# A two-layer decoder on one core: four units' context keys and values made while the router works, and three smaller edits

## The chip, the core and the metric

The kernel runs on one NeuronCore of a Trainium2 chip, as one program in one launch. The metric is the device time of an execution in microseconds (us); lower is better. A profiled execution also gives the span, from the first to the last instruction of the program on the engines.

## What is computed

The input is x, 32 sequences of 128 tokens of width 256, in f32. Each of six blocks adds its result to x:

```python
x = x + L0_attn(layernorm(x))            # latent attention, 16 heads
x = x + L0_xattn(layernorm(x), ctx, ...) # attention over ctx, with distances and a mask
x = x + L0_ffn(layernorm(x))             # 8 experts, the top 2 for each token
x = x + L1_attn(layernorm(x))            # gated scan and an MLP
x = x + L1_xattn(layernorm(x), ctx)      # attention over ctx
x = x + L1_ffn(layernorm(x))             # quantized, ternary weights, 3-tap convolution
```

What the change moves belongs to the fifth block: `lang_key = ctx @ W_lk.T + b_lk` and `lang_value = ctx @ W_lv.T + b_lv`. They depend on the inputs alone, so they may be made at any time before layer 1 reads them.

## The kernel before

**Stages.** x stays in SBUF for the whole run. `attention` (L248) does both attentions of layer 0 and, group by group of four sequences, the routing logits (`route`, L555). `phase_c` (L696) turns these into a plan for the experts, gathers tokens and runs the experts. `layer1` (L978) runs 16 units of two sequences (256 tokens) in a hand-written software pipeline (`PLAN`, a new unit every `STEP` = 11 rounds).

**The router** (L696 to L820). Two matmuls (`counts` and `totals`, L712 and L714) add up who chose which expert (`both`, written at L591). A chain of small VectorE instructions makes from them the experts' ranges, the expert of each of 71 columns of 128 tokens (`after`, `of`, `of_i`, L766 to L777), and each token's slot (`sl`, `col`, `rowp`, L764 to L785). Then 64 matmuls on one-hot tiles `onr` (L791) and `onc` (L795, scaled by ScalarE at L799) write `tokens` (L800), from which `who` and `whither`, the indices of the gathers and scatters, are made (L805 to L820).

**Contexts** (`context`, L638). One unit's context takes three pieces: `load` brings cT, 256 columns of the transposed context; `keys` is four f32 matmuls, which TensorE executes as eight instructions (tile `ck`), and two ScalarE activations that add the bias and write one half of the tile `kvc`; `values` is again eight TensorE instructions (`cv`), one VectorE add of a bias row and the store to the scratch tensor `ckv`. Of 16 units, 6 are made between the router and the experts (L829), 5 after the experts (L930), 5 within layer 1. `kvc` has four buffers, cT five. Their weights are loaded at L704 into `wc`.

**Experts.** 40 items in a list, in the repeated order of two items of two columns (256 tokens) and one of one column, two short items in a row never. `brought` (L839) reads the item's expert from `of_i`, loads its weights in two parts on SyncE's queue (tiles `moe0`, 1024 KB, and `moe1`, 1156 KB, two buffers each) and gathers the tokens on GpSimd's queue. `tokens` transposes them (PSUM `xs`, copied to `xTs` by VectorE), `first_layer` makes `h` and `second_layer` makes `y`, which a scatter on GpSimd's queue takes to `ys`. In pass j of the loop the weights of item j + 1 are asked for. At j = 1 stand the loads of layer 1's weights, `wd` (`load_d`, L688: two transfers of 1792 KB) and `wf` (L915, 2048 KB). At j = 3 stand `ternary` (L935), which adds up |wf| on VectorE, divides and rounds, and four ScalarE scalings of `wd` (L926). `wd` lies in the buffer that layer 0's weights, `wab` (L107), hold before.

**Order.** A scheduler orders each engine's instructions by its own simulated times, so one that is ready early may move ahead of others in the program. `mm` and `turned` (L206 and L209) pin a TensorE instruction behind all that was written before it for that engine with `tc.keep_in_program_order`; so do the stores to `ckv` and the fetches of `yr` on SyncE's queue. The matmuls at L712, L714, L800 and L945, the loads of `wd` and `wf`, and almost all work of the other engines are free. An instruction on an engine or queue waits at its head for all that it needs, and what is behind it waits too.

**Rows of scales** (`on_rows`, L1084). To lay 128 per-token scales along the free axis, a matmul takes the scale column, broadcast to 128 columns, as weights and the identity as moving operand; two calls for each unit, two blocks each.

Of the kernel before, what the change touches and what calls it, by code (L numbers as in the profile page):

```python
# [10 lines left out]
F32 = mybir.dt.float32  # L11
# [6 lines left out]
P = 128  # L18
# [58 lines left out]
def decoder(ctx: ExitStack, tc: tile.TileContext, a: dict, out: bass.AP):  # L77
# [28 lines left out]
    nc.sync.dma_start(out=rv, in_=a["rv"][:RV_A].partition_broadcast(P))  # L106
    wab = wpool.tile([P, AB_W], F32, tag="w1", name="wab")  # L107
    nc.sync.dma_start(out=wab[:, :A_W], in_=a["wab"][:, :A_W])
    for g in range(1, NG):
        load_x(g)  # L110
    nc.sync.dma_start(out=wab[:, A_W:], in_=a["wab"][:, A_W:])
    qpos_i = const.tile([P, NB], I32, name="qpos_i")
# [128 lines left out]
    def conr(name):  # L241
        at, w = C_AT[name]
        return cstr[:, at - C_W : at - C_W + w]

    def attention():  # L248
        with tc.tile_pool(name="pa", bufs=2) as pool, tc.tile_pool(name="pa1", bufs=1) as keep:
# [363 lines left out]
            for _ in group_a(0):  # L613
                pass
            slots = (
                (a_scores, 0), (b_scores, 0), (ahead, 0), (a_weights, 1), (b_turned, 2),
# [20 lines left out]

    def context(u, wcs, turned_tile, kv_tile):  # L638

        wc = wcs.rearrange("p (w c m) -> p w c m", w=2, c=2)  # L640
        t = {}

        def load():
            t["cT"] = turned_tile(f"cT_k{u}")
            nc.sync.dma_start(
                out=t["cT"], in_=a["ctxT"][:, u * T : (u + 1) * T].rearrange("(c p) t -> p c t", p=P)
            )

        def keys():
            t["kv"] = kv_tile(f"kvc_{u}")  # L650
            p = bank(f"ck_{u}").rearrange("p (c t) -> p c t", c=2)
            for c in range(2):
                for k in range(2):
                    mm(p[:, c, :], wc[:, 0, k, c * P : (c + 1) * P], t["cT"][:, k, :], k == 0, k == 1)
            for c in range(2):
                A.activation(
                    t["kv"][:, 0, c * T : (c + 1) * T], p[:, c, :], AF.Identity, bias=vec("b_lk")[:, c : c + 1]
                )

        def values():  # L660
            p = bank(f"cv_{u}").rearrange("p (i d) -> p i d", i=U)
            for i in range(U):
                for c in range(2):
                    mm(p[:, i, :], t["cT"][:, c, i * S : (i + 1) * S], wc[:, 1, c, :], c == 0, c == 1)
            V.tensor_tensor(
                t["kv"][:, 1].rearrange("p (i d) -> p i d", i=U), p,
                row("b_lv")[:, None, :].to_broadcast([P, U, D]), ALU.add,
            )
            tc.keep_in_program_order(nc.sync.dma_start(out=ckv[u], in_=t["kv"]))

        return load, keys, values

    CTX_FIRST, CTX0 = 6, 11

# [13 lines left out]
    def load_d():  # L688
        w = wpool.tile([P, D_W], F32, tag="w1", name="wd")
        for k in range(2):  # L690
            h = D_W // 2
            nc.sync.dma_start(out=w[:, k * h : (k + 1) * h], in_=a["wd"][:, k * h : (k + 1) * h])
        return w


    def phase_c():  # L696


        with (
# [11 lines left out]
            bothf = both.rearrange("p t e -> p (t e)")  # L711
            PE.matmul(pc[:, : NB * NE], lhsT=upper, rhs=bothf, start=True, stop=True)  # L712
            pt = bank("totals")
            PE.matmul(pt[:, : NB * NE], lhsT=ones_b, rhs=bothf, start=True, stop=True)  # L714
            k = lambda name, sh, dt=F32: keep.tile([P, *sh], dt, name=name)
# [49 lines left out]

            after = pool.tile([P, NHC * TS], F32, tag="hTs", name="after")[:, : 2 * NE * NJ]  # L766
            after = after.rearrange("p (q e) -> p q e", e=2 * NE)
            V.tensor_tensor(
                after, conr("iota")[:, :NJ, None].to_broadcast([P, NJ, 2 * NE]),
                ends.rearrange("p k e -> p (k e)")[:, None, :].to_broadcast([P, NJ, 2 * NE]), ALU.is_ge,  # L770
            )
            of, of2 = k("of", (NJ,)), k("of2", (NJ,))
            V.tensor_reduce(of, after, AX.X, ALU.add)
            V.tensor_scalar(of2, of, float(NE), -float(NE), ALU.is_ge, ALU.mult)
            V.tensor_tensor(of, of, of2, ALU.add)
            of_i = k("of_i", (NJ,), I32)
            V.tensor_scalar(of_i, of, float(NE - 1), None, ALU.min)  # L777
# [10 lines left out]
            for t in range(0, NB, G):  # L788
                for j in range(2):
                    o = pool.tile([P, G, P], F16, tag="onr", name=f"onr_{t}_{j}", bufs=3)  # L790
                    V.tensor_tensor(  # L791
                        o, conr("iota")[:, None, :].to_broadcast([P, G, P]), bc(rowp[:, j, t : t + G], P), ALU.is_equal
                    )
                    c = pool.tile([P, G, NJ], F16, tag="onc", name=f"onc_{t}_{j}", bufs=3)
                    V.tensor_tensor(  # L795
                        c, conr("iota")[:, None, :NJ].to_broadcast([P, G, NJ]), bc(col[:, j, t : t + G], NJ), ALU.is_equal
                    )
                    for i in range(G):
                        A.activation(c[:, i, :], c[:, i, :], AF.Copy, scale=conr("tok")[:, t + i : t + i + 1])  # L799
                        PE.matmul(  # L800
                            pk[j][:, :NJ], lhsT=o[:, i, :], rhs=c[:, i, :],
                            start=t + i == 0, stop=t + i == NB - 1,
                        )

            two = k("two", (2, NJ))  # L805
            for j in range(2):
# [13 lines left out]
            V.tensor_copy(whither, tkn)  # L820

            contexts = [
                context(
                    u, wcs, lambda n: cpool.tile([P, 2, T], F32, tag="cT", name=n, bufs=5),
                    lambda n: cpool.tile([P, 2, U * D], F32, tag="kv", name=n, bufs=4),
                )
                for u in range(CTX0)
            ]
            for pieces in contexts[:CTX_FIRST]:  # L829
                for piece in pieces:  # L830
                    piece()
            for pieces in contexts[CTX_FIRST:]:
                pieces[0]()
            wf = keep.tile([P, 4096], F32, name="wf")
# [4 lines left out]
            def brought(q, n):  # L839
                e = nc.sync.value_load(of_i[0:1, q : q + 1], min_val=0, max_val=NE - 1)  # L840
                w = []
# [69 lines left out]
            for j in range(len(order)):  # L911
                following = brought(*order[j + 1]) if j + 1 < len(order) else None
                if j == 1:
                    wd = load_d()
                    nc.sync.dma_start(out=wf, in_=a["wf"])  # L915
                now = first_layer(t)
                t = tokens(following) if following else None
                second_layer(now)
                if j == 3:
                    ternary(wf, keep)  # L920
                    for c in range(2):
                        for part, v in (
                            (wd[:, c * 1280 : (c + 1) * 1280], "n1"),
                            (wd[:, 3072 + c * FF : 3072 + (c + 1) * FF], "n2"),
                        ):
# [4 lines left out]
            for pieces in contexts[CTX_FIRST:]:  # L930
                for piece in pieces[1:]:
                    piece()
        return wd

    def ternary(wf, keep):  # L935

        ones = keep.tile([P, P], F32, name="ones")
        V.memset(ones, 1.0)
        asum = small.tile([P, 2], F32, tag="asum", name="asum")
        for k in range(2):  # L940
            V.tensor_reduce(
                asum[:, k : k + 1], wf[:, k * 2048 : (k + 1) * 2048], AX.X, ALU.add, apply_absolute_value=True
            )
        pa = bank("asum")
        PE.matmul(pa[:, 0:2], lhsT=ones, rhs=asum, start=True, stop=True)  # L945
        V.tensor_scalar(wm, pa[:, 0:2], 1.0 / (D * FF), 1e-5, ALU.mult, ALU.max)
# [31 lines left out]
    def layer1(wd):  # L978
# [8 lines left out]
        with (  # L987
# [441 lines left out]
            for u in range(CTX0, NU):  # L1429
                for piece, r in zip(  # L1430
                    context(
                        u, wcs, lambda n: sb("d", n, 4), lambda n: sb("kv", n, 2, shape=(2, U * D)),
                    ),
                    CTX_ROUNDS[u - CTX0],
                ):
                    between.setdefault(r, []).append(piece)
            units = [unit(u) for u in range(NU)]
# [117 lines left out]
```

## Time and profile before

| | |
|---|---|
| three runs | 1924.77, 1928.21, 1928.52 us; median 1928.21 |
| the profiled execution: time / span | 1926.33 us / 1924.5 us |
| mean granted TensorE clock | 0.944 |
| busy share of the span: TensorE / VectorE / ScalarE / GpSimd | 91% / 58% / 56% / 21% |
| attention of layer 0, with the routing logits | 0 to 607.9 us |
| router, to the last `tokens` matmul | 607.9 to 639 us |
| six contexts on TensorE | 639 to 661.4 us |
| experts | 663.2 to 1150 us |
| layer 1 | 1150 to 1924.5 us |

PE is TensorE (PEld its weight loads), DVE is VectorE, ACT is ScalarE, POOL is GpSimd and SP is SyncE, whose queue issues most transfers. In rows of the chain the columns are start, duration, and engine, tile and line; the chain leads back from the last instruction, at each step to what released it. In rows by stretch each engine has its busy time and, in brackets, its instructions, then follow the granted clock, the mean busy share of the DMA engines and GB/s. A matmul's end is modelled, so a busy TensorE need not be at its peak.

### The profile page before, as it was taken

To read this page: it belongs to the slowest core of one execution; us is meant where nothing else is said; L and a number is where in the kernel's file an instruction comes from. 1 tells how busy PE (TensorE), PEld (TensorE's weight loads), DVE (VectorE), ACT (ScalarE), POOL (GpSimd) and SP (SyncE) were. 2 spreads that over 40 slices of the span, in tenths; PEclk is the share of its full clock that TensorE was granted. 3 is DMA by queue.
4 is the path that set the end of the run, shared out by engine and by line. 5 is a ranking of instruction groups with operands and counts; after the bars stand their busy time and mean duration, and the time that the engine had idled before them with its cause. 6 is when DMAs were issued, how large, how long until landed. Compare 5 with 4: busy or idle time off the path is not lost.

```text
span 1924.5 us, 33253 instructions
## 1 busy us (share of the span) xinstructions
PE 1751.5 (91%) x12400; PEld 1436.3 (75%) x12400; DVE 1124.8 (58%) x3769; ACT 1068.3 (56%) x2376; POOL 405.9 (21%) x409
## 2 busy tenths in 40 slices
PE   6999998998985999999999999999899989999853
PEld 3777766766764789888888888787787777788742
DVE  6787776777777421101111104456788888888797
ACT  3565558888883522222222224546776676677662
POOL 4111000000000222222222211222332332333221
PEclk8999989999897899999999999999999999999975
DMA  5000010111003766766666635100001000010000
GB/s 164 2 2 2 13 34 23 44 46 45 12 12 129 271 221 226 238 209 218 223 239 210 232 105 178 52 22 23 23 28 50 28 28 28 28 34 17 28 13 21
DMA packets 58387, 169.59 MB, mean 88 GB/s; under 512 B 6256, under 2 KB 35312, under 8 KB 47472
## 3 DMA queue, kind: packets, MB, share of 16 engines
q1 hardware_dynamic: 51696, 149.61, 23.1%
q0 software_dynamic: 6528, 17.83, 2.4%
q8 instruction: 99, 1.62, 0.3%
q14 instruction: 64, 0.52, 0.1%
HBM read 141.73 MB, written 25.69 MB: 87 GB/s over the span
## 4 chain that ended last, share of the span: by engine, by line
PE 54%; DVE 25%; ACT 10%; POOL 5%; DMA 4%; issue 2%; SPq 0%; POOLq 0%; DVEq 0%; ACTq 0%
PE h L207 12%; PE y L207 12%; ACT sd_b L536 3%; DMA yr<-ys 3%; DVE top_f L1376 2%; DVE sd_b L526 2%; PE st_a L207 2%; DVE z_f L1357 2%; PE s_a L207 2%; PE y_a L207 2%; PE q_d L207 2%; PE od_a L207 2%; POOL z_f L1363 2%; PE et_b L210 1%; PE q_a L207 1%
## 5 line engine op out<-in xcount | busy, mean ns | idle before, releaser
L876 ACT ACTIVATE hTs<-h,moe 128x256 f32<-128x256 f32 (+1 forms) x320 | 141.3, 441 | 340.6 <-PE h L207 331.5
L207 PE MATMUL h<-xTs,moe 128*128 128x256 f32 (+1 forms) x1280 | 243.0, 348 | 1.0 <-DVE xTs L864 1.0
L207 PE MATMUL y<-moe,hTs 128*128 128x256 f32 x1088 | 241.4, 379 | 0.0
L207 PEld LDWEIGHTS h<-xTs,moe 128*128 128x128 f32 x1280 | 214.9, 191 | 24.9 <-DVE xTs L864 1.2
L207 PEld LDWEIGHTS y<-moe,hTs 128*128 128x128 f32 x1088 | 203.7, 190 | 26.1
L536 ACT ACTIVATE sd_b<-sd_b,nan_b 128x128 f32<-128x128 f32 x512 | 153.1, 390 | 29.7 <-DVE nan_b L533 29.7
L864 DVE COPY xTs<-xs 128x512 f32<-128x512 f32 (+1 forms) x40 | 24.4, 610 | 221.3 <-PE xs L210 221.3
L888 DVE TENSOR_TENSOR yt<-y,moe 128x256 f32<-128x256 f32 x68 | 28.8, 424 | 205.5 <-PE y L207 205.5
L526 DVE CUSTOM_DVE_ANT_0 sd_b<-nd_b,s_b 128x128 f32<-128x128 f32 x512 | 112.0, 281 | 19.7 <-PE s_b L207 19.5
L207 PE MATMUL m_m<-wd,sT_m 128*128 128x256 f32 x512 | 119.8, 382 | 0.0
L1363 POOL TENSOR_TENSOR z_f<-z_f,e_f 128x508 f32<-128x508 f32 x64 | 71.7, 1120 | 220.4 <-DVE z_f L1357 101.7
L207 PE MATMUL f_m<-hT_m,wd 128*128 128x256 f32 x512 | 118.0, 386 | 0.0
L850 POOL DMA_INDIRECT xr<-xs,who x68 | 65.9, 970 | 223.5 <-PE xs L210 181.5
L207 PEld LDWEIGHTS f_m<-hT_m,wd 128*128 128x128 f32 x512 | 97.1, 194 | 13.1 <-issue 0.5
L889 POOL DMA_INDIRECT ys<-yt,whither x68 | 67.4, 991 | 185.8 <-DVE yt L888 183.3
L207 PEld LDWEIGHTS m_m<-wd,sT_m 128*128 128x128 f32 x512 | 96.1, 192 | 12.7 <-ACT sT_m L1223 0.2
L145 POOL TENSOR_TENSOR rs_c<-ve_c,mhalf 128x4 f32<-128x4 f32 x8 | 8.1, 1011 | 406.4 <-DVE ve_b L143 281.3
L1347 ACT ACTIVATE z_f<-d_f,pv 128x256 f32<-128x256 f32 x128 | 70.3, 590 | 34.9 <-DVE d_f L1342 34.9
L1370 ACT ACTIVATE z_f<-z_f 128x512 f32<-128x512 f32 x64 | 40.3, 630 | 80.4 <-POOL z_f L1363 80.4
L443 DVE TENSOR_REDUCE nm<-s_a 128x4 f32<-128x512 f32 x128 | 78.9, 676 | 5.4 <-PE s_a L207 5.3
L473 ACT ACTIVATE et_a<-st_a 128x512 f32<-128x512 f32 x128 | 66.4, 613 | 19.0 <-PE st_a L207 19.0
L207 PE MATMUL s_b<-kEO_b,qT_b 32*128 32x256 f32 x512 | 57.4, 435 | 20.6 <-ACT kEO_b L312 16.4
(370 smaller groups left out, 3840.9 us busy)
## 6 DMA issues: line engine op xcount, KB each, us to landing
moe<-in_moe SPq DMA_DIRECT2D x40, 1156.0 KB
moe<-in_moe SPq DMA_DIRECT2D x40, 1024.0 KB
ckv<-kvc SPq DMA_DIRECT2D x16, 512.0 KB
yr<-ys SPq DMA_DIRECT2D x32, 256.0 KB
kv_e<-ckv SPq DMA_DIRECT2D x16, 512.0 KB
x<-in_x SPq DMA_DIRECT2D x8, 512.0 KB
cT_b<-in_ctxT SPq DMA_DIRECT2D x8, 512.0 KB
xs<-xn_c SPq DMA_DIRECT2D x8, 512.0 KB
```

The source lines that it names most:

```text
L207: tc.keep_in_program_order(PE.matmul(out, lhsT=lhsT, rhs=rhs, start=start, stop=stop))
L443: V.tensor_reduce(nms[i % 2][:, at : at + 2 * (P - HD)].rearrange("p (e x) -> p x e", e=2)[:, :2, :], sp[r], AX.X, ALU.max, negate=True,)
L473: A.activation(et[:, r].rearrange("p j q -> p (j q)"), st[r], AF.Exp)
L526: V.tensor_tensor_reduce(sd[:, r, j, :], nd[:, i, :], sp[r][:, j, :], SLOPES[head(r, j)], -3e38, ALU.add, ALU.max, mx[:, 4 * r + j : 4 * r ...
L536: A.activation(sd[:, r, j, :], sd[:, r, j, :], AF.Exp, bias=nan[:, 4 * r + j : 4 * r + j + 1])
L850: GP.indirect_dma_start(out=xr[h], out_offset=None, in_=xs[:, :], in_offset=bass.IndirectOffsetOnAxis(ap=who[:, q + h : q + h + 1], axis=0),)
L876: A.activation(hT[:, hc, : n * P], p, AF.Relu, bias=b1[:, hc : hc + 1])
L889: GP.indirect_dma_start(out=ys[:, :], out_offset=bass.IndirectOffsetOnAxis(ap=whither[:, q + h : q + h + 1], axis=0), in_=yt[:, h, :], in_ ...
L1347: A.activation(o["z"][:, hc, :], o["d", k][:, j, :], AF.Identity, scale=cw[:, hc, 1:2], bias=cb[:, hc : hc + 1],)
L1357: V.scalar_tensor_tensor(z[:, :, 1:], d[:, j, :].rearrange("p (b t) -> p b t", b=U)[:, :, : S - 1], cw[:, hc, 0:1], z[:, :, 1:], ALU.mult, ...
L1363: GP.tensor_tensor(z[:, :, : S - 1], z[:, :, : S - 1], e.rearrange("p h (b t) -> p (h b) t", b=U)[:, :, 1:], ALU.add,)
L1370: A.activation(z, z, AF.Silu)
```

## The change

1. **Four contexts early.** `context` is split into making and keeping, and moves ahead of `attention`. The buffer of `wab` is declared at the width of `wd`. `load_early`, called in `attention` after the first group's preparation, brings the context weights and the cT of units 0 to 3 into its free columns. Context 0's 16 TensorE instructions stand at the end of `attention`, ahead of `counts`; its keeping and contexts 1 to 3 stand right behind `totals`; contexts 4 and 5 stay where six were. For units 0 to 3 ScalarE copies `cv` out of PSUM and GpSimd adds the bias row, in place of one VectorE add. `counts`, `totals`, `tokens` and the matmul of `ternary` are now pinned.
2. **Layer 1's weights.** The loads of `wd` and `wf` move from j = 1 to j = 2, and those of `wd` are pinned. `ternary` is parted: the sums of |wf| (`weight_sums`) stand at j = 4, pinned on VectorE, and the product, the rounding and the scalings of `wd` at j = 6.
3. **The experts of the columns.** In place of one comparison and one sum over 71 x 16 elements, the 28 pairs of columns are compared with 8 ends (224 elements) and the last 15 columns with 16 (240).
4. **Rows of scales** are made by transposes (`turned`) in place of matmuls.

```diff
-    wab = wpool.tile([P, AB_W], F32, tag="w1", name="wab")
+    wab = wpool.tile([P, D_W], F32, tag="w1", name="wab")
...
+        def values_kept(by_vector=True):
+            v, b = t["kv"][:, 1].rearrange("p (i d) -> p i d", i=U), row("b_lv")[:, None, :].to_broadcast([P, U, D])
+            if by_vector:
+                V.tensor_tensor(v, t["v"], b, ALU.add)
+            else:
+                A.copy(v, t["v"])
+                GP.tensor_tensor(v, v, b, ALU.add)
+            tc.keep_in_program_order(nc.sync.dma_start(out=ckv[u], in_=t["kv"]))
...
+    CTX_EARLY, CTX_FIRST, CTX0 = 4, 6, 11
+    def load_early():
+        at = AB_W
+        wcs = wab[:, at : at + E_W // 2]
+        nc.sync.dma_start(out=wcs, in_=a["we"][:, E_W // 2 :])
+        at += E_W // 2
+        for u in range(CTX_EARLY):
+            cT = wab[:, at + u * 2 * T : at + (u + 1) * 2 * T].rearrange("p (c t) -> p c t", c=2)
+            early.append(context(u, wcs, lambda n, cT=cT: cT, lambda n: kept_in[0](n)))
+            early[u]["load"]()
...
             for _ in group_a(0):
                 pass
+            load_early()
...
+            early[0]["keys_made"]()
+            early[0]["values_made"]()
...
-            PE.matmul(pc[:, : NB * NE], lhsT=upper, rhs=bothf, start=True, stop=True)
+            mm(pc[:, : NB * NE], upper, bothf, True, True)
...
+            early[0]["keys_kept"]()
+            early[0]["values_kept"](False)
...
+            for c in contexts[CTX_EARLY:CTX_FIRST]:
+                c["load"]()
+            for c in contexts[1:4]:
+                c["keys"]()
+                c["values_made"]()
+                c["values_kept"](False)
...
+            V.tensor_tensor(
+                after2, iota[:, : 2 * NT : 2, None].to_broadcast([P, NT, NE]),
+                ends[:, 0, None, :].to_broadcast([P, NT, NE]), ALU.is_ge,
+            )
+            V.tensor_reduce(pairs_of, after2, AX.X, ALU.add)
...
-            for pieces in contexts[:CTX_FIRST]:
-                for piece in pieces:
-                    piece()
-            for pieces in contexts[CTX_FIRST:]:
-                pieces[0]()
+            for c in contexts[4:6]:
+                c["keys"]()
+                c["values"]()
+            for c in contexts[CTX_FIRST:]:
+                c["load"]()
...
-                if j == 1:
+                if j == 2:
                     wd = load_d()
                     nc.sync.dma_start(out=wf, in_=a["wf"])
...
-                if j == 3:
-                    ternary(wf, keep)
+                if j == 4:
+                    summed = weight_sums(wf, keep)
+                if j == 6:
+                    ternary(wf, *summed)
...
-                    mm(p[:, i * S : (i + 1) * S], v[:, i : i + 1].to_broadcast([P, P]), ident, True, True)
+                    turned(p[:, i * S : (i + 1) * S], v[:, i : i + 1].to_broadcast([P, P]))
```

More of the change, by code (lines that the diff above doesn't have):

```diff
@@ L110, in decoder @@
         load_x(g)
-    nc.sync.dma_start(out=wab[:, A_W:], in_=a["wab"][:, A_W:])
+    nc.sync.dma_start(out=wab[:, A_W:AB_W], in_=a["wab"][:, A_W:])
     qpos_i = const.tile([P, NB], I32, name="qpos_i")
@@ L243, in conr, with context, load, keys_made @@
         return cstr[:, at - C_W : at - C_W + w]
+    def context(u, wcs, turned, kv_tile):
+        wc = wcs.rearrange("p (w c m) -> p w c m", w=2, c=2)
+        t = {}
+        def load():
+            t["cT"] = turned(f"cT_k{u}")
+            nc.sync.dma_start(
+                out=t["cT"], in_=a["ctxT"][:, u * T : (u + 1) * T].rearrange("(c p) t -> p c t", p=P)
+            )
+        def keys_made():
+            t["k"] = p = bank(f"ck_{u}").rearrange("p (c t) -> p c t", c=2)
+            for c in range(2):
+                for k in range(2):
+                    mm(p[:, c, :], wc[:, 0, k, c * P : (c + 1) * P], t["cT"][:, k, :], k == 0, k == 1)
+        def keys_kept():
+            t["kv"] = kv_tile(f"kvc_{u}")
+            for c in range(2):
+                A.activation(
+                    t["kv"][:, 0, c * T : (c + 1) * T], t["k"][:, c, :], AF.Identity, bias=vec("b_lk")[:, c : c + 1]
+                )
+        def values_made():
+            t["v"] = p = bank(f"cv_{u}").rearrange("p (i d) -> p i d", i=U)
+            for i in range(U):
+                for c in range(2):
+                    mm(p[:, i, :], t["cT"][:, c, i * S : (i + 1) * S], wc[:, 1, c, :], c == 0, c == 1)
+        def values_kept(by_vector=True):
[6 more added lines that the diff above has]
+            tc.keep_in_program_order(nc.sync.dma_start(out=ckv[u], in_=t["kv"]))
+        def keys():
+            keys_made()
+            keys_kept()
+        def values():
+            values_made()
+            values_kept()
+        return dict(locals())
+    CTX_EARLY, CTX_FIRST, CTX0 = 4, 6, 11
+    early = []
+    def load_early():
[7 more added lines that the diff above has]
+            early[u]["load"]()
+    kept_in = []
     def attention():
@@ L636, in attention @@
                     pass
[L638 to L673, printed above, removed]
+            early[0]["keys_made"]()
+            early[0]["values_made"]()
     first_made = []
@@ L691, in load_d @@
             h = D_W // 2
-            nc.sync.dma_start(out=w[:, k * h : (k + 1) * h], in_=a["wd"][:, k * h : (k + 1) * h])
+            tc.keep_in_program_order(nc.sync.dma_start(out=w[:, k * h : (k + 1) * h], in_=a["wd"][:, k * h : (k + 1) * h]))
         return w
@@ L711, in phase_c @@
             bothf = both.rearrange("p t e -> p (t e)")
-            PE.matmul(pc[:, : NB * NE], lhsT=upper, rhs=bothf, start=True, stop=True)
+            mm(pc[:, : NB * NE], upper, bothf, True, True)
             pt = bank("totals")
-            PE.matmul(pt[:, : NB * NE], lhsT=ones_b, rhs=bothf, start=True, stop=True)
+            mm(pt[:, : NB * NE], ones_b, bothf, True, True)
+            kept_in.append(lambda n: cpool.tile([P, 2, U * D], F32, tag="kv", name=n, bufs=4))
+            early[0]["keys_kept"]()
+            early[0]["values_kept"](False)
+            contexts = early + [
+                context(u, wcs, lambda n: cpool.tile([P, 2, T], F32, tag="cT", name=n, bufs=5), kept_in[0])
+                for u in range(CTX_EARLY, CTX0)
+            ]
+            for c in contexts[CTX_EARLY:CTX_FIRST]:
[4 more added lines that the diff above has]
+                c["values_kept"](False)
             k = lambda name, sh, dt=F32: keep.tile([P, *sh], dt, name=name)
@@ L764, in phase_c @@
             V.tensor_reduce(sl, picks, AX.X, ALU.add)
-            after = pool.tile([P, NHC * TS], F32, tag="hTs", name="after")[:, : 2 * NE * NJ]
-            after = after.rearrange("p (q e) -> p q e", e=2 * NE)
+            iota = conr("iota")
+            of = k("of", (NT + NJ - 2 * NT,))
+            pairs_of, ones_of = of[:, :NT], of[:, NT:]
+            n1 = NJ - 2 * NT
+            after = pool.tile([P, NHC * TS], F32, tag="hTs", name="after")
+            after2 = after[:, : NT * NE].rearrange("p (q e) -> p q e", e=NE)
+            after1 = after[:, NT * NE : NT * NE + n1 * 2 * NE].rearrange("p (q e) -> p q e", e=2 * NE)
             V.tensor_tensor(
-                after, conr("iota")[:, :NJ, None].to_broadcast([P, NJ, 2 * NE]),
-                ends.rearrange("p k e -> p (k e)")[:, None, :].to_broadcast([P, NJ, 2 * NE]), ALU.is_ge,
-            )
[L772 to L776, printed above, removed]
+                after2, iota[:, : 2 * NT : 2, None].to_broadcast([P, NT, NE]),
+                ends[:, 0, None, :].to_broadcast([P, NT, NE]), ALU.is_ge,
+            )
+            V.tensor_reduce(pairs_of, after2, AX.X, ALU.add)
+            V.tensor_tensor(
+                after1, iota[:, 2 * NT : NJ, None].to_broadcast([P, n1, 2 * NE]),
+                ends.rearrange("p k e -> p (k e)")[:, None, :].to_broadcast([P, n1, 2 * NE]), ALU.is_ge,
+            )
+            V.tensor_reduce(ones_of, after1, AX.X, ALU.add)
+            of2 = k("of2", (n1,))
+            V.tensor_scalar(of2, ones_of, float(NE), -float(NE), ALU.is_ge, ALU.mult)
+            V.tensor_tensor(ones_of, ones_of, of2, ALU.add)
+            of_i = k("of_i", (NT + n1,), I32)
             V.tensor_scalar(of_i, of, float(NE - 1), None, ALU.min)
@@ L799, in phase_c @@
                         A.activation(c[:, i, :], c[:, i, :], AF.Copy, scale=conr("tok")[:, t + i : t + i + 1])
[L800 to L803, printed above, removed]
+                        mm(pk[j][:, :NJ], o[:, i, :], c[:, i, :], t + i == 0, t + i == NB - 1)
             two = k("two", (2, NJ))
@@ L820, in phase_c @@
             V.tensor_copy(whither, tkn)
[L822 to L828, printed above, removed]
-            for pieces in contexts[:CTX_FIRST]:
-                for piece in pieces:
-                    piece()
-            for pieces in contexts[CTX_FIRST:]:
-                pieces[0]()
+            for c in contexts[4:6]:
[3 more added lines that the diff above has]
+                c["load"]()
             wf = keep.tile([P, 4096], F32, name="wf")
@@ L839, in brought @@
             def brought(q, n):
-                e = nc.sync.value_load(of_i[0:1, q : q + 1], min_val=0, max_val=NE - 1)
+                at = q // 2 if n == 2 else q - NT
+                e = nc.sync.value_load(of_i[0:1, at : at + 1], min_val=0, max_val=NE - 1)
                 w = []
@@ L928, in phase_c, with weight_sums, ternary @@
             first_made.append(fetch(0))
-            for pieces in contexts[CTX_FIRST:]:
-                for piece in pieces[1:]:
-                    piece()
+            for c in contexts[CTX_FIRST:]:
+                c["keys"]()
+                c["values"]()
         return wd
-    def ternary(wf, keep):
+    def weight_sums(wf, keep):
         ones = keep.tile([P, P], F32, name="ones")
-        V.memset(ones, 1.0)
+        tc.keep_in_program_order(V.memset(ones, 1.0))
         asum = small.tile([P, 2], F32, tag="asum", name="asum")
         for k in range(2):
-            V.tensor_reduce(
-                asum[:, k : k + 1], wf[:, k * 2048 : (k + 1) * 2048], AX.X, ALU.add, apply_absolute_value=True
-            )
+            tc.keep_in_program_order(
+                V.tensor_reduce(
+                    asum[:, k : k + 1], wf[:, k * 2048 : (k + 1) * 2048], AX.X, ALU.add, apply_absolute_value=True
+                )
+            )
+        return ones, asum
+    def ternary(wf, ones, asum):
         pa = bank("asum")
-        PE.matmul(pa[:, 0:2], lhsT=ones, rhs=asum, start=True, stop=True)
+        mm(pa[:, 0:2], ones, asum, True, True)
         V.tensor_scalar(wm, pa[:, 0:2], 1.0 / (D * FF), 1e-5, ALU.mult, ALU.max)
@@ L1429, in layer1 @@
             for u in range(CTX0, NU):
[L1430 to L1436, printed above, removed]
+                made = context(u, wcs, lambda n: sb("d", n, 4), lambda n: sb("kv", n, 2, shape=(2, U * D)))
+                for what, r in zip(("load", "keys", "values"), CTX_ROUNDS[u - CTX0]):
+                    between.setdefault(r, []).append(made[what])
             units = [unit(u) for u in range(NU)]
```

## The prediction, made before the changed kernel was run

> **What bounds the kernel now.** I read the busy time by stretch first, for which engine fills each stage; then the chain that ended last, between 607 and 664 us; then the timeline of the router and of one unit of layer 1; then SyncE's issues among the experts.
>
> ```profile
> 601.70:607.90 6.20, 5.88 (x24) 5.04 (x24) 0.95 (x3) 1.17 (x2) 0.00 (x0) 0.50 0.24 85
> 607.90:639.00 31.10, 14.34 (x66) 6.78 (x67) 28.51 (x87) 18.85 (x68) 0.31 (x1) 0.50 0.91 345
> 639.00:661.40 22.40, 22.40 (x97) 19.43 (x97) 9.68 (x16) 6.95 (x14) 5.91 (x6) 0.92 0.78 268
> 663.20:1150.00 486.80, 486.40 (x2504) 433.51 (x2505) 59.74 (x115) 141.26 (x320) 125.51 (x129) 1.00 0.62 211
> ```
>
> In the router VectorE is full (28.5 of 31.1 us) and TensorE has little to do, at a granted clock of 0.50. Then TensorE alone is full with six contexts, and it stays full to the end of the experts. So TensorE work moved from the third stretch into the second shortens the run, less what it adds to VectorE's chain.
>
> ```profile
> 610.75 0.15 DVE both L591
> 610.95 0.37 PE counts L712
> 611.32 0.23 PE totals L714
> 611.57 0.44 DVE tot L717
> ...
> 616.09 1.25 DVE after L768
> 617.83 1.24 DVE of L773
> ...
> 639.12 3.62 PE ck L207 x8
> 642.74 1.73 PE cv L207 x8
> 644.47 1.73 PE ck L207 x8
> ...
> 662.52 0.61 DVE xTs L864
> 663.17 7.17 PE h L207 x32
> ```
>
> The chain runs through VectorE and two short matmuls to the last `tokens` matmul at 639.1, then through six contexts back to back, and 1.8 us after them the first expert starts (663.17). The first eight `ck` instructions take 3.62 us, at half clock; later blocks of eight take 1.73.
>
> **The sum, to the start of the first expert.**
>
> (a) Four contexts leave the full stretch: 4 x (1.73 + 1.73) = **-13.8 us**. The two that stay bear the cold start that the first bears now.
>
> (b) Context 0 stands ahead of `counts` on TensorE. It can start when the routing logits end, 607.9. Its 16 instructions take 3.62 + 1.73 = 5.35 us if the clock rises as at 639, and end at 613.2, where `both` is ready at 610.9: 2.3 us late, less 0.1 as `counts` and `totals` then run warm: **+2.2**. Bounds: all warm, 3.46 us, +0.4; all cold, 7.2 us, +4.2. I take the middle because 5.9 us of transposes and 8-column matmuls in 601.7 to 607.9 left the clock at 0.50. Behind this wait stands VectorE's whole chain.
>
> (c) The experts of the columns: 1.25 + 1.24 us become four instructions of 224 to 240 elements; the nearest, 256 elements (`slot`, L758), takes 0.33 in the chain: 4 x 0.31 = 1.24, and two followers on 15 elements, not 71, save 0.1: **-1.35**.
>
> (d) Four bias adds of 128x512 on GpSimd, beside a VectorE that has no slack. GpSimd's add of this shape in layer 1 (L1192) takes 1.27 us. What it does to VectorE stands in the timeline of a unit:
>
> ```profile
> 1478.49 1.47 DVE L1290 TENSOR_SCALAR at_e<-at_e,den_e 128x128 f32<-128x128 f32 x2
> ...
> 1515.18 1.28 POOL L1156 TENSOR_TENSOR u_d<-u_d,v_d 128x512 f32<-128x512 f32 x1 [3.73 <-ACT v_d L1154]
> 1515.25 1.82 DVE L1398 TENSOR_SCALAR zi_f<-z_f 128x512 bf16<-128x512 f32 x2
> ```
>
> The first of the two `zi_f` (0.41 alone) lasts to the end of the add, 1.07 us more; the pair at 1478 waits likewise for another add. By my count over the whole trace a VectorE instruction is drawn out by over 0.3 us beside 6 of 16 adds of L1156, 10 of 16 of L1166, 1 of 16 of L1192, none of L1212. The adds will fall at about 614, 618, 621 and 625, inside the chain. VectorE is busier there than in layer 1, and nearly all its instructions read SBUF only, so I take three hits in four at 1.0: **+3.0**; bounds 0 and 4 x 1.1 = 4.4. The Trainium skill, "SBUF — State Buffer", section "Who interferes with whom", speaks against the change here: the pair of ports that GpSimd uses is locked for a whole instruction, and a VectorE instruction with two SBUF inputs waits. By its rule each of the four adds could cost its full length, an estimate of 5.1 us.
>
> (e) ScalarE: a context's keeping is 0.84 us for the keys plus a copy of 128x512, 0.58 (L290). Today ScalarE waits 4.7 us for `wd` here and is idle until 622.5; with `wd` gone the four fit, the last at about 624, beside the start of `onc` (622.5, then some 626): 0, bound +1.4. Contexts 1 to 3 take 10.4 us warm on TensorE, 613.6 to 624, and `tokens` is pinned behind them; its first one-hot tile comes at about 623.1 + 2.2 - 1.35 + 2 = 626. TensorE is in time by 2 us.
>
> Sum: -13.8 + 2.2 - 1.35 + 3.0 = **-9.95**. The router's end moves by +3.85, to 643; contexts 4 and 5 end at 639.1 + 3.85 + 3.62 + 3 x 1.73 = 651.8. Late next would be the gathers: `who` at 644.3, the second gather's issue 1.5 us later, some 2.4 us to land (scatters in the chain take 2.4): 648.5, hidden by 3 us. Expert 0's weights are asked for behind four `ckv` stores, the last at about 626; 2.2 MB at the 419 GB/s of 626 to 638 land by 633, hidden.
>
> **The experts** stay full on TensorE if weights come in time.
>
> ```profile
> 684.63 0.33 SPq L844 DMA_DIRECT2D moe<-in_moe  x1
> 692.31 0.33 SPq L844 DMA_DIRECT2D moe<-in_moe  x1
> 695.33 4.68 SPq L844 DMA_DIRECT2D moe<-in_moe  x2
> ```
>
> On the clock of before, `wd` goes out right behind item 3's second part (692.3), and item 4's first part (695.3) lands behind it; item 4 starts at 713.55. `wf` is free, was issued at 625.0 although its place is later, and I expect that again. Then 1.18 + 3.67 + 1.05 = 5.9 MB at 419 GB/s take 14.1 us, and with 1.4 us of latency land at 707.8: hidden by 5.7 us. With `wf` behind `wd` it is 8.0 MB, 712.8: hidden by under 1 us. Price: 0. The two sums (2.28 us each, L941) follow item 4's `y`; the next `xTs` is wanted after item 5's 3.6 + 3.5 us: hidden by 2.5 us less the copy's 0.7. The four scalings (2.6 + 2.2 us on ScalarE, 29% busy) and the rounding are as large as before: 0. Should ScalarE wait at its head for a late `wd`, as it did for 4.7 us at 610, TensorE runs on into free PSUM banks; I bound this by +3.
>
> **Rows of scales.** Four instructions (`rows_f`, 0.61) become two (0.38, the pair of `pt_e` beside it): 0.23 x 32 calls = 7.3 us of TensorE. But in a unit's 42.5 us the chain goes through the fetch of `yr`, VectorE, GpSimd and ScalarE, and TensorE idles 2.8 us for `hT_d`; of the chain's matmuls only `q_d` and `a_d` weigh. **-0.5**, for the drain; bounds -7.3 and 0. The skill's "TensorE: Matmul & The Clock Gate", section "Terms", has the f32 transpose mode four times as fast, where these rows give 0.61 against 0.38; by the rule 11 us of TensorE would go, an estimate, equally off the chain. The scheduler may order layer 1's free instructions anew: 0, bounds -3 and +3 from the 2.8 us of idle time for each unit.
>
> **Total** -9.95 - 0.5 = **-10.5 us**. The profiled execution's 1926.3 us (span 1924.5, 1.8 around it) become 1915.8; it lay 1.9 under the median 1928.2, so I expect a median of **1917.5 us**.
>
> **Rivals.**
>
> 1. *The router's chain eats the gain* (about the same time, within 0.2%, which is 3.9 us and about what a measurement here can tell from no change). If the clock stays at 0.50 through all four contexts, they and the two short matmuls last 4 x 7.2 + 0.6 = 29.4 us, to 637.3; `tokens`, which starts at 623.1 today, is pinned behind them and starts 14.2 us late, and -13.8 + 14.2 leaves +0.4: 1928.6. For it: 0.50 in all of 607.9 to 639. Against: at 642.7 the clock rose after 3.6 us of dense f32 matmuls, which these are.
>
> 2. *Layer 1's weights starve the experts* (slower). `wd` and `wf`, until now hidden in the router, lie ahead of item 4's first part. If they run at the stage's mean 211 GB/s, not 419, 8.0 MB take 38 us, item 4 starts at 731.7, 18 us late, and the total is +7.7: 1936. It decides from a stall of 10.5 us on, that is under some 265 GB/s. For it: 283 GB/s in 692 to 706. Against: those shares were waits for requests; when busy the queue moved 351 to 419.
>
> 3. *More than I think:* TensorE's 7.3 us in layer 1 count, and GpSimd's adds hit nothing: -13 - 7.3 = -20: 1908.
>
> **How the numbers follow.** Forecast (-6.5 to -15): 0.70. Rival 1, or delays that add up to it: 0.12. Rival 2: 0.10. Rival 3: 0.08. Faster takes the forecast, rival 3 and 0.01 of rival 1: 0.79; same 0.10; slower, rival 2 and 0.01 of rival 1: 0.11. The forecast's own range is 1913 to 1922. The given one takes in half of rivals 1 and 3: 1909 to 1925.
>
> **What would show it.** Right: `ck` and `cv` of four units on TensorE between 607.9 and 627; `counts` near 613; VectorE instructions of over 1 us beside four GpSimd adds; 16 context instructions for each of two units ahead of the first `h`, which starts near 653; the experts' stretch still 487 us with TensorE full; layer 1 still near 774. Wrong: idle TensorE at item 4 or 5, a granted clock of 0.50 past 613, or a stretch of layer 1 that differs by over 3 us.

## The result, and the profile after

Four runs of the changed kernel gave 1904.37 to 1910.32 us, median **1906.52**, against 1927.03 for four of the kernel before: ratio 0.9897, 95% interval 0.9877 to 0.9916. That is 20.5 us less where 10.5 were forecast, and below the range (1909). The profiled execution took 1910.32 us, its span 1908.5.

| us, profiled executions | before | after | |
|---|---|---|---|
| last `r_c` to the start of `counts` | 3.1 | 5.7 | +2.6 |
| last `r_c` to the first `h` | 55.3 | 47.8 | -7.5 |
| first `h` to the last `h` | 479.2 | 479.2 | 0 |
| first `q_d` (L1133 before) to the end of the span | 756.3 | 743.7 | **-12.6** |

`r_c`, the routing logits, ended at 607.9 before and at 612.0 after. Over 14 profiles this end lies between 603.0 and 614.7 us although TensorE, VectorE and ScalarE have the same order there; so stages are compared by their own lengths, not by the clock time at which they lie. The spans of the two profiled executions differ by 16.0 us: 7.5 and 12.6 less in these stages, 4.1 more in the attention.

By stretch after (the columns are those of the rows shown of before): the router with four contexts, the two that stay, the experts, layer 1.

```profile
612.00:648.50 36.50, 30.16 (x131) 20.29 (x131) 31.39 (x88) 21.65 (x77) 6.21 (x5) 0.73 0.75 263
648.50:659.80 11.30, 10.30 (x37) 8.36 (x37) 3.81 (x12) 1.68 (x4) 6.86 (x7) 0.75 0.66 220
659.80:1146.00 486.20, 486.03 (x2502) 433.32 (x2502) 63.83 (x118) 145.42 (x324) 125.45 (x128) 1.00 0.63 219
1164.80:1908.50 743.70, 642.14 (x3308) 541.96 (x3308) 567.04 (x1435) 480.13 (x918) 216.52 (x204) 0.94 0.10 35
```

The router's TensorE time went from 14.3 to 30.2 us and the full stretch behind it from 22.4 to 11.3; the experts are as full as before. In the router's timeline after, TensorE reaches `counts` late, and each GpSimd add (two of the four are shown) has a VectorE instruction beside it that took 0.17 to 0.69 us before:

```profile
617.68 0.27 PE L207 MATMUL counts<-both,upper 128*128 128x256 bf16 x1
...
618.54 1.26 POOL L282 TENSOR_TENSOR kvc<-kvc,rv 128x512 f32<-128x512 f32 x1 [6.15 <-ACT kvc L281]
618.63 1.72 DVE L770 TENSOR_TENSOR_SCAN run<-allone,tot 128x256 f32<-128x256 f32 x1
622.22 1.26 POOL L282 TENSOR_TENSOR kvc<-kvc,rv 128x512 f32<-128x512 f32 x1 [2.41 <-ACT kvc L281]
622.25 1.25 DVE L785 SCALAR_TENSOR_TENSOR left<-pairs,cols 128x8 f32<-128x8 f32 x1
```

In layer 1 a unit took 42.3 to 43.6 us before (from `q_d` to `q_d`, units 7 to 14) and 40.9 to 41.9 after. Nothing in the prediction says why, and the experiments begin there.

### The profile page after: what moved, and what is told of

Same layout as the page of the kernel before. It is cut to its first block, busy times and chain, and to the rows that moved or that the text cites. A ratio compares the mean times of both kernels' runs of the same rounds, so it can differ in the third digit from the quotient of the medians.

```text
span 1908.5 us, 33114 instructions
## 1 busy us (share of the span) xinstructions
PE 1744.7 (91%) x12336; PEld 1427.5 (75%) x12336; DVE 1124.4 (59%) x3767; ACT 1069.7 (56%) x2380; POOL 410.2 (21%) x413
## 4 chain that ended last, share of the span: by engine, by line
PE 54%; DVE 27%; ACT 8%; POOL 4%; DMA 3%; issue 2%; SPq 0%; POOLq 0%; DVEq 0%; ACTq 0%
PE h L207 12%; PE y L207 12%; ACT sd_b L604 3%; DVE top_f L1433 3%; DMA yr<-ys 3%; DVE z_f L1414 2%; DVE sd_b L594 2%; PE st_a L207 2%; PE et_b L210 2%; PE y_a L207 2%; PE s_a L207 2%; PE od_a L207 2%; PE m_m L207 1%; PE s_b L207 1%; DVE z_f L1454 1%
```

## The experiments

Ratios are to the kernel before on the same chip. The table has the two stage lengths of each profile; the texts on record follow.

| kernel | ratio, 95% interval | `r_c` to `h` | `q_d` to the end |
|---|---|---|---|
| rows_alone | 0.9951 [0.9933, 0.9969] | 55.6 | 745.4 |
| order_alone | 0.9953 [0.9934, 0.9972] | 55.6 | 745.7 |
| rows_late | 1.0022 [1.0002, 1.0041] | 55.6 | 756.2 |
| rows_back | 0.9977 [0.9959, 0.9995] | 47.8 | 759.5 |
| ctx0_late | 0.9906 [0.9876, 0.9936] | 45.4 | 742.7 |
| bias_pe | 0.9900 [0.9869, 0.9932] | 48.1 | 745.8 |
| bias_dve | 0.9896 [0.9864, 0.9928] | 44.9 | 743.3 |
| yr_first | 0.9890 [0.9851, 0.9928] | 47.9 | 742.9 |
| all_three | 0.9931 [0.9907, 0.9954] | 51.1 | 745.4 |
| yr_pinned | 0.9853 [0.9822, 0.9883] | 47.4 | 732.4 |
| yr_ctx0 | 0.9845 [0.9814, 0.9876] | 45.4 | 729.2 |
| yr_ctx0_bias | 0.9847 [0.9816, 0.9879] | 45.1 | 732.1 |

**Where layer 1's 12.6 us come from.** Between the two programs, VectorE's order in layer 1 differs in one thing over and over: `d_f_0`, a multiply of the quantized FFN, stands in eight units ahead of the first gate instruction of the unit four places on, not behind it. ScalarE's order changes with it: in the same units `z_f`, which is made from `d_f`, goes ahead of an activation, `sT_m`, that stood before it. "The order" below means both; no run parts them. Four kernels take the cheap rows and this order apart.

rows_alone (the kernel before and this):

```diff
-                    mm(p[:, i * S : (i + 1) * S], v[:, i : i + 1].to_broadcast([P, P]), ident, True, True)
+                    turned(p[:, i * S : (i + 1) * S], v[:, i : i + 1].to_broadcast([P, P]))
```

> The kernel before with the rows of scales as transposes and nothing else. The order of VectorE's instructions changes by itself: in eight units of layer 1 (7 to 14) the multiply d_f_0 of the unit four places back stands ahead of the first of the two gate instructions instead of between them. From the first q_d to the end of the span was 756.3 us before and 743.7 after the whole change. Theory T1 (TensorE's shorter rows shorten layer 1 directly) and theory T2 (the order that the cheaper rows bring about does it) both expect 744, and a time 12.6 us under the kernel before (ratio 0.9935). Theory T3 (the gain in layer 1 comes from the contexts made early or from another part) expects 756 and no change.

order_alone (the kernel before; rows stay matmuls; `gated` holds the second gate instruction, and the last line stands ahead of the taps):

```diff
-                    V.scalar_tensor_tensor(o["pre"], o["ga"], 1.0, o["pre"], ALU.add, ALU.mult)
+                    if 7 <= u <= 14:
+                        with tc.issue_after(firsts[u - 4]):
+                            V.scalar_tensor_tensor(o["pre"], o["ga"], 1.0, o["pre"], ALU.add, ALU.mult)
...
+                        with tc.issue_after(gated[u + 4]) if k == 0 and 3 <= u <= 10 else nullcontext():
```

> The kernel before, rows as matmuls as they were, but in units 7 to 14 the first gate instruction is queued behind d_f_0 of the unit four places back, and the taps of that unit behind the second gate instruction: VectorE's order of the kernel with transposed rows, on the dear rows. T2 expects 744 us from the first q_d to the end and 12.6 us less in all (8 units at 1.6). T1 expects 756 and no change. If each has a share, the time says which.

rows_late (rows_alone, but the multiply is written between the two gate instructions):

```diff
+                    gated = V.scalar_tensor_tensor(o["pre"], o["ga"], 1.0, o["pre"], ALU.add, ALU.mult)
+                    if late_d:
+                        with tc.issue_after(gated.ins):
+                            late_d.pop()()
...
+                    if k == 0 and 3 <= u <= 10:
+                        late_d.append(lambda: V.tensor_tensor(o["d", 0], h, o["rows1"], ALU.mult))
```

> The kernel before with transposed rows, but in units 7 to 14 d_f_0 is put between the two gate instructions, where it stood: the cheap rows with the order of before. T1 expects 744 us from the first q_d to the end and 12.6 us less in all; T2 expects 756 and no change, at most the 1 us of the drain.

rows_back (the changed kernel with the first diff turned round):

> The changed kernel with the rows of scales as matmuls again, as before; VectorE's order in layer 1 goes back by itself. T1 and T2: the 12.6 us come back, 8 us under the kernel before (20.5 less 12.6; ratio 0.996), 756 from the first q_d to the end. T3: layer 1 stays at 744 and the time at 20 us under the kernel before.

Measured, from the first `q_d` to the end: 745.4, 745.7, 756.2 and 759.5 us, against 756.3 before and 743.7 after. The order does it, with dear rows or cheap ones; the cheap rows with the old order gain nothing, so T1 falls, and so does T3, since the contexts are not needed for it. That the same order took 759.5 in one kernel and 756.3 in another goes with the clock described at the end: from the first `q_d` on it was at half speed for 117 us in rows_back and for 108 before. That this is the cause was not tried. The same rows in two timelines, first the kernel before:

```profile
1651.60 0.68 DVE L1191 TENSOR_TENSOR pre_d<-pre_d,qn_d 128x512 f32<-128x512 f32 x1
1652.36 1.27 POOL L1192 TENSOR_TENSOR pre_d<-pre_d,v_d 128x512 f32<-128x512 f32 x1 [0.96 <-DVE pre_d L1191]
1653.66 0.69 DVE L1195 SCALAR_TENSOR_TENSOR pre_d<-ga_d,pre_d 128x512 f32<-128x512 f32 x1 [1.38 <-POOL pre_d L1192]
1654.27 0.68 DVE L1342 TENSOR_TENSOR d_f<-h_f,rows_f_sb 128x512 f32<-128x512 f32 x1
...
1656.99 0.68 DVE L1303 TENSOR_TENSOR lv_e<-lv_e,kv_e 128x512 f32<-128x512 f32 x1
...
1657.70 0.33 SPq L1241 DMA_DIRECT2D kv_e<-ckv  x1
1658.09 0.43 SPq L684 DMA_DIRECT2D yr<-ys  x1
```

and order_alone:

```profile
1641.88 0.68 DVE L1193 TENSOR_TENSOR pre_d<-pre_d,qn_d 128x512 f32<-128x512 f32 x1
1642.48 0.68 DVE L1349 TENSOR_TENSOR d_f<-h_f,rows_f_sb 128x512 f32<-128x512 f32 x1
1642.63 1.27 POOL L1194 TENSOR_TENSOR pre_d<-pre_d,v_d 128x512 f32<-128x512 f32 x1 [0.96 <-DVE pre_d L1193]
1643.94 0.69 DVE L1199 SCALAR_TENSOR_TENSOR pre_d<-ga_d,pre_d 128x512 f32<-128x512 f32 x1 [0.78 <-POOL pre_d L1194]
...
1646.06 0.68 DVE L1309 TENSOR_TENSOR lv_e<-lv_e,kv_e 128x512 f32<-128x512 f32 x1
```

Before, VectorE sat idle for 1.38 us until GpSimd's subtraction ended, and `d_f` and what follows it (ScalarE's `z_f`, VectorE's taps) came after. With `d_f` in that gap, `lv_e` begins 4.18 us after the first row, not 5.39: **1.21 us** a unit. `lv_e` frees the buffer of `kv`, SyncE then issues `kv`, and behind it the fetch of `yr`, which VectorE and then `hT_d` wait for.

Eight units at 1.21 are 9.7 us. The rest is read from TensorE, which waits for `hT_d` ahead of `q_d`. The kernel before, then order_alone, the same unit:

```profile
1670.81 3.78 PE L207 MATMUL q_d<-hT_d,wd 128*128 128x256 f32 x8 [2.96 <-ACT hT_d L1055]
1674.39 3.10 PE L207 MATMUL a_d<-hT_d,wd 128*128 128x256 f32 x8
```

```profile
1659.83 1.99 PE L207 MATMUL q_d<-hT_d,wd 128*128 128x256 f32 x8 [1.70 <-ACT hT_d L1055]
1661.66 1.89 PE L207 MATMUL a_d<-hT_d,wd 128*128 128x256 f32 x8
```

After an idle time of 2.96 us the same 16 instructions take 3 us more. So a wait that is 1.2 us shorter often saves the clock as well. Before, one slow block alone cost little: the units that begin with the slow blocks 7 and 9 took 42.6 and 42.4 us, those with 8 and 10, at speed, 42.3 and 42.5. Units 11 to 13, slow three times in a row, took 43.5 to 43.6, some 3.3 us more together. This second part was not tried by itself.

**The router.** Two edits to the changed kernel, each against one term of the sum. ctx0_late:

```diff
-            early[0]["keys_made"]()
-            early[0]["values_made"]()
...
-            for c in contexts[1:4]:
+            for c in contexts[:4]:
```

> The changed kernel with context 0 made behind counts and totals, not ahead of them. In the changed kernel counts begins 5.8 us after the last r_c (612.0 to 617.8), before the change 3.0 us (607.9 to 610.9), and the first h 47.8 us after the last r_c. Theory A (this wait is on the chain that ends the router): counts again 3.0 us after r_c, and the first h 45.0 us after it, 2.8 us less in all. Rival B (tokens is pinned behind the four contexts, and these now start cold and later: 3.62 + 7 x 1.73 = 15.7 us from 3.7 us on, to 19.4 us after r_c, where tokens begins today): counts comes early, but tokens begins at 19.4 as before, and nothing is gained. Layer 1 at 744 from the first q_d in both.

Measured: `counts` 3.1 us after the last `r_c` and the first `h` after 45.4 us, 2.4 less, near the 2.8 of theory A. But `tokens` did begin at 19.5 us as rival B has it, and ended only 1.4 us sooner: its first twelve matmuls ran back to back, in 0.65 us, because their one-hot tiles were there. The other 1.0 us lies in the two contexts behind: the full clock came 3.7 us after their first instruction, not 5.7 us. In the whole time 2.4 us drown in the scatter.

bias_pe adds the bias as a matmul over one row:

```diff
+                if u < CTX_EARLY:
+                    mm(p[:, i, :], one_row, row("b_lv")[0:1, :], False, True)
...
-                GP.tensor_tensor(v, v, b, ALU.add)
```

> The changed kernel with the bias of the four early contexts added by TensorE (one matmul over a single row into the same PSUM bank for each half of a context), so that the four GpSimd adds go. In the changed kernel they stand beside run 1.72 us (0.69 before), left 1.25 (0.17), run 1.47 (0.41), onr 1.69 (0.68) on VectorE: 1.04 us each. Theory A (these four hits lie on the chain): 4.2 us less from the last r_c to the first h, 47.8 to some 44, less what two short matmuls ahead of counts cost (0.2 to 0.5). Rival B (another wait takes their place, such as tokens behind the contexts on TensorE, which are now longer by 8 short matmuls): 47 or more.

Measured 48.1: nothing gained. The cure cost as much as the illness, as this timeline of bias_pe shows:

```profile
623.07 1.03 PE L207 MATMUL cv<-wab 128*128 128x256 f32 x4
624.03 0.69 PE L207 MATMUL cv<-rv,one_row 1*128 1x256 f32 x2
```

One row costs 0.63 us from start to start, more than half of the 0.96 us for two matmuls over 128 rows. Eight are 5 us: `counts` came 7.3 us after `r_c`, `tokens` at 22.7 us. VectorE's instructions were at their old lengths. So the hits were tried in another way, bias_dve:

```diff
-            early[0]["values_kept"](False)
+            early[0]["values_kept"]()
...
-                c["values_kept"](False)
+                c["values_kept"]()
```

> The changed kernel with the bias of the four early contexts added by VectorE as for the other units (0.69 us each, straight from PSUM), so that ScalarE's copies and GpSimd's adds go, and with them the 4 x 1.04 us by which GpSimd's adds draw out VectorE. Theory A (the hits lie on the chain): 4.2 less 4 x 0.69 = 2.8, 1.4 us less from the last r_c to the first h: 46.4, against 47.8. Rival B (an add that stands in VectorE's order ahead of its context's end makes VectorE wait for TensorE): 48 or more. The kernel with the bias on TensorE said nothing on this, because a matmul over one row took 0.63 us, 5 us in all, and tokens waited for it.

Measured 44.9, 2.9 us less. In its timeline `run` (1.72 us above) is short again, although VectorE carries the adds:

```profile
619.37 0.69 DVE L279 TENSOR_TENSOR kvc<-cv,rv 128x512 f32<-128x512 f32 x1 [1.02 <-PE cv L207]
...
620.50 0.69 DVE L770 TENSOR_TENSOR_SCAN run<-allone,tot 128x256 f32<-128x256 f32 x1
```

The first add lies mostly in a wait and delays what follows by 0.4 us, the other three by 0.6 us each: 2.2 us in place of the four hits of 4.2. `tokens` begins 1.8 us and ends 2.3 us sooner, against `r_c`, and the contexts behind it happened to be 0.6 us shorter. So GpSimd's adds cost more than the VectorE adds that they replaced.

**Is it the fetch of `yr`?** If the loop runs through `lv_e`, `kv` and `yr`, taking `yr` out of it should gain again. yr_first moves the load of `kv` in the changed kernel:

```diff
                 def e_stats():
...
-                    o["kv"] = sb("kv", f"kv_{e_}", bufs=2, shape=(2, U * D))
-                    nc.sync.dma_start(out=o["kv"], in_=ckv[u])
...
                 def e_norm():
+                    o["kv"] = sb("kv", f"kv_{e_}", bufs=2, shape=(2, U * D))
+                    nc.sync.dma_start(out=o["kv"], in_=ckv[u])
```

> The changed kernel with a unit's kv asked for one and a half rounds later, behind the fetch of yr of the unit three places on, not ahead of it. In the changed kernel the load of kv waits for lv_e to free its buffer, the fetch of yr stands behind it on SyncE, VectorE waits 3.0 us for yr in each unit, and TensorE 1.6 us for hT_d; a unit takes 41.2 us, TensorE is busy for 37.7 to 38.2 of them. Theory A (the loop of layer 1 runs through the slot of kv, SyncE and yr; this is why the place of d_f counted): a unit at 39.5 us, layer 1 some 20 us shorter (13 units at 1.6), 724 from the first q_d, about 1886 us. Rival B (the place of x in VectorE's order, behind d_f, holds the loop as late): VectorE's wait for yr goes but the unit stays at 41.2, and the time at 1906.

Layer 1 stayed at 742.9: the scheduler had moved the adds of `yr` forward by a whole unit, right behind `lv_e` of the same pass, and VectorE waited as before, now for the next unit's rows:

```profile
1637.09 0.69 DVE L1360 TENSOR_TENSOR lv_e<-lv_e,kv_e 128x512 f32<-128x512 f32 x1
...
1638.20 0.93 SPq L719 DMA_DIRECT2D yr<-ys  x2
1641.92 0.88 DVE L1163 SCALAR_TENSOR_TENSOR x<-yr,rw,x 128x256 f32<-128x256 f32 x2 [2.91 <-DMA yr<-ys]
```

all_three joins ctx0_late, bias_pe and yr_first:

> The three edits in one kernel: context 0 behind counts and totals, the bias of the early contexts on TensorE, the fetch of yr ahead of kv. If each of their first theories holds, 44 - 2.8 = 41 us from the last r_c to the first h and 724 from the first q_d, in all some 27 us under the changed kernel: 1880. If tokens then waits for the four contexts (3.7 + 15.7 + 8 short matmuls, to some 21 us after r_c, where it began at 19.4), the router stays at 47 to 48, and the time is 1886.

It was the slowest of them: with context 0 late and the one-row matmuls, the four contexts ended 25.7 us after `r_c`, `tokens` waited for them, and the first `h` came after 51.1 us. Edits that each move work on TensorE do not add up when one wait joins them.

yr_pinned holds the adds in their place as well:

```diff
-                    for k, y in enumerate(o.pop("yr")):
+                    with tc.issue_after(kept_lv[u - 5]) if u >= 5 else nullcontext():
+                        for k, y in enumerate(o.pop("yr")):
```

> The kernel with the fetch of yr ahead of kv had the same 41.2 us a unit, but in it the adds of yr onto x moved forward by a whole unit in VectorE's order, so that the fetch of the next unit again was asked for right ahead of its use and VectorE still waited 2.9 us for it. Here the fetch stands ahead of kv and the adds are queued behind lv_e of the unit five places back, where they were. Theory A (lv_e frees kv, kv lets the fetch go, the fetch holds VectorE: the loop that d_f stood in): yr is there long before, VectorE's 3 us wait goes, and a unit falls to 38.2 to 39.8 us, layer 1 to 715 to 730 from the first q_d, 1877 to 1892 us in all. Rival B (the loop is held elsewhere, and d_f's place counted for another reason, such as GpSimd's taps that wait for z_f): a unit stays at 41 and the time at 1906.

Measured: 39.9 us a unit, layer 1 at 732.4 us, 1894.5 us in all. That is theory A's way, just short of each of its ranges, and far from rival B's 41 and 1906. A window of 40 us and one unit's rows:

```profile
1624.46 2.19 DVE L1166 SCALAR_TENSOR_TENSOR x<-yr,rw,x 128x256 f32<-128x256 f32 x4
```

```profile
1636.27 1.99 PE L207 MATMUL q_d<-hT_d,wd 128*128 128x256 f32 x8 [0.35 <-ACT hT_d L1112]
```

```profile
1570.00:1610.00 40.00, 37.50 (x203) 31.80 (x202) 36.77 (x92) 29.74 (x58) 13.20 (x13) 1.00 0.10 33
```

The adds no longer wait, TensorE waits 0.35 us for `hT_d` instead of 1.4 to 2.4, and keeps its clock. Layer 1 is 11 us shorter than after the change, somewhat less than the 14 to 29 of the expectation: TensorE is now busy for 37.5 of 40 us and VectorE for 36.8, so little idle time is left to win.

The last two join this with the router's edits:

> Context 0 behind counts and totals (2.4 us less from the last r_c to the first h, as measured: 45.4) together with the fetch of yr ahead of kv and the adds queued behind lv_e. If the two gains add up and theory A on yr holds: 1875 to 1890 us. If yr gains nothing: 1904.

> The same with the bias of the early contexts on VectorE as well. If the hits of GpSimd lie on the chain here too: some 44 us from the last r_c to the first h and 1.4 us less than the kernel with two edits; if tokens now waits for the four contexts on TensorE, which end 19.5 us after the last r_c: no difference from that kernel.

They took 1896.4 and 1896.3 us, some 28 us under the kernel before; by their ratios they cannot be told from yr_pinned, and all fall short of the expected 1890, as yr_pinned did. These three beat the kernel before; against the changed kernel, which was timed in another session, the interval of yr_ctx0 is clear by a hair and the other two overlap a little, but layer 1 is 11 to 15 us shorter in all three traces. In the stages the first `h` comes 45.4 us after `r_c` again, as in ctx0_late, while the bias on VectorE adds 0.3 at most: `tokens` begins at 19.5 us in both, when the contexts end.

## Why the prediction was wrong

- **(a) Four contexts leave the full stretch, -13.8.** -12.8: from the last `tokens` to the first `h` 24.1 us became 11.3. The second block of the cold start took 2.8 us (651.92 to 654.72 below) and not 1.73: the full clock came 5.7 us after the first instruction of the two contexts, at 654.1, where it came after 3.6 us before.

```profile
648.37 3.75 PE L207 MATMUL ck<-cT_k,wc 128*128 128x256 f32 x8
651.92 2.96 PE L207 MATMUL cv<-wc,cT_k 128*128 128x256 f32 x8
654.72 1.89 PE L207 MATMUL ck<-cT_k,wc 128*128 128x256 f32 x8
```

- **(b) Context 0 ahead of `counts`, +2.2.** +2.6. Context 0 took 5.9 us, not 5.35, and `both` was ready 0.9 us before `counts` began (616.75 to 617.68). With context 0 behind `counts`, the last `tokens` came 1.4 us sooner. The middle value was nearly right.
- **(c) The experts of the columns, -1.35.** Right: the four instructions take 0.30, 0.30, 0.32 and 0.31 us to what follows each, 1.23 in all.
- **(d) Four GpSimd adds, +3.0.** +4.2: four hits of four, 1.04 us each. The rule of the Trainium skill, "SBUF — State Buffer", section "Who interferes with whom", which the prediction weighed, has all four hit, as they did. At the full length of each add its estimate, 5.1 us, lies 0.9 us above the measured cost. In three of the four, the VectorE instruction began 0.03 to 0.09 us after its add; why it lost 1.04 us of the add's 1.26 and not all of it stays open.
- **(e) ScalarE, 0.** `ex_c` stood behind the first keeping on ScalarE, VectorE waited 1.75 us for it, and `both` was ready 4.8 us after `r_c`, not 3.0. TensorE was later still, so this hid behind (b) and was not measured by itself; the prediction had not seen it.
- Sum of the router: -12.8 + 2.6 - 1.3 + 4.2 = -7.3, measured -7.5, predicted -9.95.
- **Experts, 0.** Right: 479.2 us in both.
- **Rows of scales, -0.5.** The cheap rows with the old order: 756.2 against 756.3 us, nothing. "Off the chain" was right. (The prediction's 11 us for a fourfold gain is a slip: with a quarter of 0.61 us left, 32 calls would save 14.6 us. By its own sum the median would be 1917.7, not 1917.5.)
- **The step that failed:** "The scheduler may order layer 1's free instructions anew: 0, bounds -3 and +3 from the 2.8 us of idle time for each unit." It did order them anew, and that was worth -12.6 us, the largest term of all but (a). The idle time of one unit was taken as the bound for the whole layer, though a unit is repeated 16 times and its idle time lay on a loop: a shift of 1.21 us in eight units, and in some of them the clock kept on top. It was also the sign of being wrong that the prediction named last.
- Rival 3 (1908) had nearly the right time by luck: TensorE's 7.3 us did not count, and GpSimd's adds all hit.

Rows alone (-9.4 us) and all but the rows (-4.4) add up to 13.8, not 20.5; their intervals (some 3.5 us each way) and that of the change (3.8) span the gap of 6.7 us only if the three errors add up. The stage lengths say where it lies: in the router all but the rows gained the same 7.5 us, but in layer 1 the rows alone gained 10.9 us and all but the rows lost 3.2, against 12.6 for the whole change. Each order scatters there by some 3 us, 742.7 to 745.8 with the new one and 756.2 to 759.5 with the old one.

## What to carry to other kernels

Where a scheduler places instructions by simulated times, an edit that makes one operation cheaper may be worth nothing by itself and much by the order that it brings about: compare the two programs' orders, and if a wait stands in a loop, count it once for each pass. A shared queue can close such a loop without any data between its ends; here a transfer that waited for a buffer kept an unrelated one from being issued, and moving it helped only once the consumer was held in its place too. Work given to a second engine to spare a busy one is not free if the two engines get in each other's way: four adds on GpSimd cost VectorE more than doing them itself.

## What the runs showed of the hardware

**Where a short idle time falls decides whether it costs TensorE its clock.** Take each `q_d` block of layer 1 in the 14 profiles, its eight instructions' time and the idle time ahead of it. With up to 1.9 us idle, 172 of 172 blocks took 1.89 to 2.0 us; with 1.9 to 2.95, 26 of 41 took 2.4 to 3.7; above 2.95, 11 of 11 took 2.4 to 3.8. What parts the 41 shows in the clock: in every trace all its changes lie on one grid of 3.41 us. Here are windows of this grid around two nearly equal idle times of the kernel before, 2.75 us (block 8, two rows) and 2.78 us (block 9, two rows):

```profile
1451.55:1454.96 3.41, 2.37 (x11) 1.73 (x10) 3.14 (x12) 2.21 (x5) 2.12 (x3) 1.00 0.00 0
1454.96:1458.37 3.41, 1.71 (x8) 1.53 (x9) 3.41 (x9) 3.37 (x8) 0.64 (x1) 1.00 0.00 0
1495.92:1499.33 3.41, 0.63 (x4) 0.39 (x3) 3.38 (x10) 2.17 (x6) 1.76 (x2) 1.00 0.00 0
1499.33:1502.75 3.42, 3.42 (x10) 2.71 (x9) 3.19 (x13) 2.10 (x5) 0.61 (x1) 0.50 0.00 0
```

The first idle time is split between two windows, and the clock stays. The second lies almost whole in one, which leaves TensorE busy for 0.63 of 3.41 us, and the next window is at half clock. From the first to the last `q_d` of the 14 traces, TensorE was busy for at most 0.43 of each of the 65 windows ahead of a fall, and for at least 0.42 of each of the 2232 that kept the clock. (In the attention the clock also fell behind windows that were busy for up to 0.93, so these shares hold for layer 1 alone.) The Trainium skill, "TensorE: Matmul & The Clock Gate", section "What's actually happening", has the clock fall after an idle window of about 3.4 us that runs freely. The length and the free run agree with the grid; but here a window need not be idle.

**A matmul over one row** (1x128 by 1x256, f32) took 0.63 us from start to start where one over 128 rows took 0.48.
